# Layer 2's units: matrices further ahead, taps on another queue, x normalized earlier, norms behind the next product, larger runs; and q, k, v from tiles that are loaded first

## The chip, the cores and the metric

The kernel runs on one NeuronCore of a Trainium2 chip. A core has five engines that run side by side, each with its own in-order queue: TensorE (PE, with its weight loads shown as PEld), VectorE (DVE), ScalarE (ACT), GpSimd (POOL) and SyncE (SP), which here only issues DMAs. DMAs can be issued from the queues of SP, ACT and POOL, and all of them run on the same 16 DMA engines. The metric is device time in microseconds (us), lower is better.

## The reference, cut to what matters

x has the shape (4, 384, 64, 64), in float32. Four layers follow each other, each with its input added back: `x = x + layer(group_norm(x))`. Layer 0 is attention over the 4096 positions, on the first 96 channels; layer 1 is a gated product with a filter in the Fourier domain; layer 3 is a depthwise convolution with computed kernels. The change touches the start of layer 0 and most of layer 2:

```python
# layer 0, its start: xn is normalized over the 96 channels of x[:, :96]
qkv = jnp.einsum('oc,bchw->bohw', w_qkv, xn)     # and a batch norm with given statistics
# layer 2
y3 = _bn(_dw(x, c3_w, 1), c3_g, c3_b)            # depthwise 3x3, then norm over batch and space
y5 = _bn(_dw(x, c5_w, 2), c5_g, c5_b)            # depthwise 5x5, the same
y1 = x * c1_w.reshape(1, -1, 1, 1) + c1_b.reshape(1, -1, 1, 1)
tok = _bn(kw[:, 0:1] * y3 + kw[:, 1:2] * y5 + y1, ar_g, ar_b)
...
h1 = _gelu(_bn(_pw(tok, cm_w1), cm_g1, cm_b1))   # then a second product, and gates
```

The norms of layer 2 take their mean and variance from all batches and positions of a channel, so y3 and y5 must be known whole for a channel before the sum can be formed.

## The kernel before, in words

The program is written as a list of operations on named tiles. A scheduler orders them on each engine by its own estimate of times, places tiles in buffers, and sets the semaphores. The order of the source is therefore a priority, not a fixed order; but once it is made, each engine's queue runs strictly in order, and an instruction that waits holds all behind it.

**The start (phase_a, x_norm, qkv).** `x_norm(0)` (L631) loads all 24 tiles of batch 0 (3 groups of 128 channels, 8 blocks of 512 positions), measures each with `bn_stats`, and works out mean and scale of every group of channels. `score_shifts` (L714) follows; it holds a branch on a value that is known only at run time, and nothing crosses that branch. Then `qkv` (L680) loads the first 96 channels a second time, block by block (`centered`, L645), and makes q, k and v.

**Layer 2's first half (phase_b, L1138).** The 384 channels are cut into 12 units of 32. In a unit, partitions stand for (batch, channel). For two channels at a time, a pair, `conv53` (L1297) makes both convolutions as six products of z, which holds x with positions on the partitions, with banded matrices. Around these products stand:

- `matrices53` (L1277) makes the matrices of a pair from taps and a mask: even pairs on VectorE, odd ones on GpSimd. They are made two pairs ahead and have four buffers. `taps53` (L1271) loads the taps of four pairs at once, from SP's queue.
- `unit_strips(u + 1)` (L1215) loads the next unit's x (from SP), normalizes it on ScalarE in halves, and, from unit 4 on, transposes it into z on TensorE. It takes one step at every odd n of the 16 pairs. A load or a normalization stands in the same step as the transposes that need it.
- `conv53` copies its result from PSUM into `d_o`, measures it (`bn_stats`), and stores it to memory every fourth pair from ACT's queue: one tensor for 5x5 and one for 3x3.
- `conv_norms` (L1330), at the end of a unit, works out scales and shifts for y3 and y5 with ten small matmuls and a chain through VectorE and ScalarE.
- `unit_tok(u - 1)` (L1366) takes one step at every even n: it loads the convolutions of the unit before as (batch, channel) rows, with runs of 512 bytes, forms the sum in `d5`, with its statistics, and stores it to `tok`.

After the last unit come its tokens, the statistics over all units (`tok_stats`), and the next stage (phase_ef), whose first large products need both.

Of the kernel before, what the change touches and what calls it, by code (L numbers as in the profile page):

```python
# [28 lines left out]
NJ = 3  # L29
# [11 lines left out]
UNITS = C // 32  # L41

# [238 lines left out]
class _Builder:  # L281
    def __init__(self, ctx, tc, ins, out):
# [32 lines left out]
        self.d53 = [  # L315
            [self.dram.tile([32, B, 32, P], F32, tag=f"d{i}{u}", name=f"d_{i}_{u}") for u in range(UNITS)]
            for i in range(2)
        ]
# [189 lines left out]
    def phase_a(self, strips):  # L508
# [3 lines left out]
        with ExitStack() as ctx:  # L512
# [8 lines left out]
            self.probs = attention.enter_context(tc.tile_pool(name="a_probs", bufs=2, side="right"))  # L521
            self.center = self.const(cp, "center", PD)
# [8 lines left out]
            for k in ("r0", "m0", "n0"):  # L531
                setattr(self, k, cp.tile([P, NJ, B], F32, tag=k, name=k))
            self.qkv_weights(cp)
            for _ in self.x_norm(0):
                pass
# [6 lines left out]
            for _ in self.qkv(0, q, k4, vt):  # L542
                pass
# [87 lines left out]
    def x_norm(self, b):  # L631

        st = self.stats_tile("x_st")
        for i in range(8):
            for j in range(NJ):

                x = self.wk("x_in", "xs", 2) if b else self.big.tile([P, 512], F32, tag="q", name="x_in0", bufs=9)
                self.nc.sync.dma_start(x, self.ins["x"][b][:, j, i * 512 : (i + 1) * 512])
                self.nc.vector.bn_stats(st[:, j, i, :], x)
            yield 0.5  # L640
# [4 lines left out]
    def centered(self, b, i):  # L645
# [4 lines left out]
        nc.sync.dma_start(x, self.ins["x"][b][0:PD, 0, i * 512 : (i + 1) * 512])  # L650
        nc.vector.tensor_scalar(
            x, x, self.m0[0:PD, 0, b : b + 1], self.r0[0:PD, 0, b : b + 1], ALU.subtract, ALU.mult
# [27 lines left out]
    def qkv(self, b, q, k4, vt):  # L680
# [3 lines left out]
        xc[0] = self.centered(b, 0)  # L684
        yield 1.0
        xn[0] = self.layer_norm(xc[0])
        xc[1] = self.centered(b, 1)
        yield 2.0
        for i in range(8):
            if i + 2 < 8:  # L690
                xc[i + 2] = self.centered(b, i + 2)
                yield 1.0
# [34 lines left out]
    def maxima(self, b):  # L727
# [3 lines left out]
        q = []  # L731
        k = [self.probs.tile([P, 2048], F32, tag="p", name="mx_k") for _ in range(2)]
        for i in range(8):
# [3 lines left out]
            q.append(self.big.tile([P, 512], F32, tag="q", name="mx_q", bufs=9))  # L737
# [400 lines left out]
    def phase_b(self):  # L1138
# [5 lines left out]
        with ExitStack() as ctx:  # L1144
# [12 lines left out]
            for n in range(4):  # L1157
                self.matrices53(n)
# [4 lines left out]
            self.unit_x = [[] for _ in range(UNITS)]  # L1163
            for u in range(UNITS):
                st = self.bt_p.tile([P, 2, 16, 6], F32, tag="st", name="st")
                strips = self.unit_strips(u + 1) if u + 1 < UNITS else iter(())
                tok = self.unit_tok(u - 1) if u else self.unit_strips(0)
                nets = iter(()) if u else self.nets(cp)
                for n in range(16):
                    if u or n > 1:  # L1170
                        self.matrices53(16 * u + n + 2)
                    self.conv53(u, n, st)
                    next(strips if n % 2 else tok, None)
                    if n % 3 == 2:
                        next(nets, None)
                self.conv_norms(u, st)
# [38 lines left out]
    def unit_strips(self, u):  # L1215
# [3 lines left out]
        for i in range(2):  # L1219
            x = self.bx_p.tile([P, 2048], F32, tag="x", name="unit_x")  # L1220
            for b in range(B):
                nc.sync.dma_start(
                    x[32 * b : 32 * b + 32], self.x1[b][32 * q : 32 * q + 32, j, i * 2048 : (i + 1) * 2048]
                )
            self.unit_x[u].append(x)
            for h in range(4):
                if h % 2 == 0:
                    xh = x[:, 512 * h : 512 * h + 1024]
                    nc.scalar.activation(
                        xh, xh, AF.Identity, bias=self.norm_u[:, 1, u : u + 1], scale=self.norm_u[:, 0, u : u + 1]  # L1230
                    )
                if j:
                    m = self.pm("strip_m")
                    for k in range(4):
                        at = (4 * h + k) * P
                        nc.tensor.transpose(m[:, k * P : (k + 1) * P], x[:, at : at + P], self.ident)
                    at = 1 + 16 * i + 4 * h
                    zv = self.z[:, 32 * q : 32 * q + 32, at : at + 4, :]
# [796 lines left out]
```

## Time and profile before

| | us |
|---|---|
| median of 3 runs | 4879.94 |
| the runs | 4866.37 to 4882.83 |
| the profiled execution | 4868.55 |
| its span | 4866.7 |

| stage of the span | from, us | to, us | what |
|---|---|---|---|
| start | 0 | 41 | statistics, weights, branch |
| layers 0 and 1 | 41 | 2478 | attention, the Fourier products |
| layer 2's units | 2478 | 3041 | 12 units: first product to last |
| between | 3041 | 3088 | last tokens, statistics, gates |
| the rest | 3088 | 4867 | layer 2's large products, layer 3 |

The page divides the span in 40 slices and gives each engine's busy share in tenths. A row of a group or of the timeline names the line, the engine, the operation and its tiles, and, in brackets, how long the engine was idle before it and what ended that. Rows of waits give the total us, how often, and the longest. TensorE is busy 91% of the span, VectorE 60%, ScalarE 41%, GpSimd 15%. In the window of the units the DMA engines moved 172.50 MB in 133,702 packets, of which 104,916 were under 2 KB.

### The profile page before, as it was taken

How to read it: one execution, taken by the hardware profiler on the slowest of the kernel's cores; microseconds unless marked ns; L12 is line 12 of the kernel's file. 1: busy time of each engine (PE TensorE's matmuls, PEld its weight loads, DVE VectorE, ACT ScalarE, POOL GpSimd, SP SyncE). 2: the span in 40 equal slices, each digit the busy share in tenths (PEclk: the TensorE clock that was granted, in tenths of full speed). 3: DMA queues.
4: the chain of work that ended last, by engine and by line, in shares of the span. 5: the costliest groups of instructions: out<-in, count | busy, mean ns of one | idle time of the engine just before them, and what ended most of it. 6: DMA issues, size and time to landing. Idle time of an engine off the chain costs nothing. (4 is left out here: it accounts for less than half of the span.)

```text
span 4866.7 us, 49663 instructions
## 1 busy us (share of the span) xinstructions
PE 4413.5 (91%) x18441; PEld 2456.1 (50%) x18441; DVE 2901.2 (60%) x4642; ACT 1998.2 (41%) x2974; POOL 728.9 (15%) x594
## 2 busy tenths in 40 slices
PE   6899999999999999988978889699999997778888
PEld 2233444344443444435468888344444443667888
DVE  6766566655566455566867778555521113667898
ACT  3454344444444443436345556211133334753321
POOL 1000000000000000000034445000000001225544
PEclk8999999999999999999989989899999998788999
DMA  4211212121211111113259999866664444895776
GB/s 159 79 51 48 80 65 72 46 79 33 75 55 67 48 52 52 64 51 124 73 176 296 280 286 308 279 254 253 239 236 151 156 156 160 314 341 185 230 255 232
DMA packets 345857, 749.23 MB, mean 154 GB/s; under 512 B 22684, under 2 KB 172295, under 8 KB 336647
## 3 DMA queue, kind: packets, MB, share of 16 engines
q1 hardware_dynamic: 279864, 471.92, 31.3%
q0 software_dynamic: 32640, 151.28, 7.9%
q10 hardware_dynamic: 33102, 122.77, 6.5%
q8 instruction: 149, 2.44, 0.2%
q14 instruction: 102, 0.83, 0.1%
HBM read 443.62 MB, written 302.25 MB: 153 GB/s over the span
## 5 line engine op out<-in xcount | busy, mean ns | idle before, releaser
L788 ACT ACTIVATE probs<-sc_s 128x1024 f32<-128x1024 f32 x512 | 496.8, 1020 | 690.6 <-PE av L898 588.2
L898 PE MATMUL av<-probs,vt 128*128 128x512 f32 x1536 | 714.9, 602 | 0.0
L1097 DVE SCALAR_TENSOR_TENSOR acc<-band,vecs,acc 128x512 f32<-128x512 f32 x708 | 496.4, 746 | 45.2 <-POOL band L1058 40.0
L1591 PE MATMUL h_m<-f_h,cm_w_t 128*128 128x512 f32 x1152 | 497.4, 595 | 7.4 <-ACT f_h L1579 7.4
L1308 PE MATMUL conv_m<-toep,z 128*128 128x192 f32 (+1 forms) x2304 | 447.0, 356 | 17.8 <-DVE toep L1289 17.6
L898 PEld LDWEIGHTS av<-probs,vt 128*128 128x128 f32 x1536 | 275.6, 191 | 338.1 <-issue 334.4
L1308 PEld LDWEIGHTS conv_m<-toep,z 128*128 128x128 f32 x2304 | 410.9, 198 | 41.0 <-issue 10.1
L1905 PE MATMUL conv_m<-toep,z 128*128 128x128 f32 x3072 | 393.6, 286 | 37.9 <-POOL toep L1892 19.6
L1905 PEld LDWEIGHTS conv_m<-toep,z 128*128 128x128 f32 x3072 | 379.3, 202 | 39.9 <-POOL toep L1892 19.9
L1537 PE MATMUL h_s<-e_tok,cm_w_t 128*128 128x512 f32 x768 | 363.3, 596 | 4.2 <-DVE e_tok L1522 4.2
L1591 PEld LDWEIGHTS h_m<-f_h,cm_w_t 128*128 128x128 f32 x1152 | 219.8, 191 | 285.0 <-issue 273.9
L780 PE MATMUL sc_s<-q,k 32*128 32x512 f32 x2048 | 310.7, 644 | 19.4 <-ACT probs L788 19.1
L1599 DVE BATCH_NORM_STATS2 h_st<-f_h 128x6 f32<-128x512 f32 x96 | 66.4, 693 | 429.9 <-ACT f_h L1598 429.9
L1289 POOL TENSOR_TENSOR toep<-w,band 128x1280 f32<-128x1280 f32 x94 | 272.2, 2900 | 307.0 <-PE conv_m L1308 201.1
L1020 PE MATMUL t_m<-w_in_t,xb 128*128 128x384 f32 x768 | 279.7, 499 | 4.3 <-DVE coef L1037 4.1
L934 PE MATMUL proj_m<-xm,w_proj_t 128*128 128x512 f32 x576 | 271.6, 611 | 4.9 <-DVE xm L873 4.9
L1544 ACT COPY e_h<-h_s 128x1024 f32<-128x1024 f32 x96 | 97.2, 1012 | 400.3 <-PE h_s L1537 400.3
L1546 DVE BATCH_NORM_STATS2 h_st<-e_h 128x6 f32<-128x512 f32 x192 | 123.5, 685 | 203.8 <-ACT e_h L1544 203.8
L1537 PEld LDWEIGHTS h_s<-e_tok,cm_w_t 128*128 128x128 f32 x768 | 146.6, 191 | 188.7 <-issue 183.3
L941 DVE SCALAR_TENSOR_TENSOR x_res<-proj_m,bn_c,x_res 128x512 f32<-128x512 f32 x96 | 71.8, 748 | 241.0 <-PE proj_m L934 240.8
L1020 PEld LDWEIGHTS t_m<-w_in_t,xb 128*128 128x128 f32 x768 | 143.3, 193 | 142.0 <-issue 60.7
L1537 PE MATMUL h_s<-z,cm_w_t 128*128 128x512 f32 x384 | 196.1, 592 | 0.0
(408 smaller groups left out, 6383.4 us busy)
## 6 DMA issues: line engine op xcount, KB each, us to landing
d<-d_o ACTq DMA_DIRECT2D x96, 512.0 KB
c_d<-d SPq DMA_DIRECT2D x96, 512.0 KB
hid<-e_h ACTq DMA_DIRECT2D x16, 3072.0 KB
f_h<-hid SPq DMA_DIRECT2D x16, 3072.0 KB
x_in<-in_x SPq DMA_DIRECT2D x96, 256.0 KB
x_res<-in_x SPq DMA_DIRECT2D x32, 768.0 KB
xa<-x_res POOLq DMA_DIRECT2D x32, 768.0 KB, 3.7
xa_out<-xa SPq DMA_DIRECT2D x32, 768.0 KB
```

The lines of the kernel that those rows point to most:

```text
L780: nc.tensor.matmul(s[:, g], lhsT=k4[32 * g : 32 * g + 32, c], rhs=q[i][32 * g : 32 * g + 32], start=True, stop=True,)
L788: nc.scalar.activation(p[:, h * 1024 : (h + 1) * 1024], s[:, 2 * h : 2 * h + 2].rearrange("p a b -> p (a b)"), AF.Exp, scale=0.25,)
L898: nc.tensor.matmul(av[0], lhsT=vt[:, 4 * c + v, :], rhs=p[:, v * 512 : (v + 1) * 512], start=c == 0 and v == 0, stop=c == 7 and v == 3,)
L934: nc.tensor.matmul(m, lhsT=self.w_proj[:, j, o * P : (o + 1) * P], rhs=xm[:, j], start=j == 0, stop=j == NJ - 1,)
L1020: nc.tensor.matmul(m[:, 0:C], lhsT=xb[:, j], rhs=self.w_in[:, j, :], start=j == 0, stop=j == NJ - 1,)
L1097: nc.vector.scalar_tensor_tensor(out, src(j, k), w, done, ALU.mult, ALU.add)
L1289: eng.tensor_tensor(t, self.w53[:, at : at + 160].rearrange("p (m n) -> p m n", n=8).unsqueeze(2).to_broadcast([P, 20, 8, 8]), band.rearra ...
L1308: nc.tensor.matmul(m[:, c * 256 + to : c * 256 + to + 64 * (k1 - k0)], lhsT=self.z_[:, at : at + P], rhs=t[:, 10 * c + k0 : 10 * c + k1].r ...
L1537: nc.tensor.matmul(s[:, v, :], lhsT=w1[:, j, o * P : (o + 1) * P], rhs=t[j][:, v * 512 : (v + 1) * 512], start=j == 0, stop=j == NJ - 1,)
L1546: nc.vector.bn_stats(st[:, o, 8 * b + 2 * i + v, :], h[:, o, v * 512 : (v + 1) * 512])
L1591: nc.tensor.matmul(m, lhsT=w2[:, o, j * P : (j + 1) * P], rhs=h[:, o, v * 512 : (v + 1) * 512], start=o == 0, stop=o == 5,)
L1905: nc.tensor.matmul(m[:, ch * P : (ch + 1) * P], lhsT=self.z_[:, at : at + P], rhs=t[:, 8 * c + 2 * i : 8 * c + 2 * i + 2].rearrange("p m a ...
```

## The change

Layer 2's units: `LEAD = 3` sets the matrices three pairs ahead, with five buffers, and five are made before the first pair. The taps' loads are issued from GpSimd's queue and have three buffers instead of two. `unit_strips` becomes a generator that loads and normalizes one step before it yields; the first step of unit u + 2 is taken at the end of unit u, and each load is cut in two along the positions. `conv_norms` of a unit is called behind the first pair of the next one. The token steps are taken at n = 2, 4, ..., 14 and 15 instead of 0, 2, ..., 14. The two convolutions lie beside each other in one tensor, `d_o` and `d53` alike, so that a store writes 8 KB a row and a load reads runs of 1 KB; the sum is written over the unit's x (`o`) instead of over `d5`, and stored from there.

The start: eight tiles (the first 128 channels) are loaded first of all and kept; `first_norm` works out mean and scale of the 96 channels alone; after the branch, `qkv` reads the kept tiles; the other 16 tiles are measured behind it. In `maxima`, inside the branch, q takes another buffer.

```diff
+LEAD = 3
-        self.d53 = [
-            [self.dram.tile([32, B, 32, P], F32, tag=f"d{i}{u}", name=f"d_{i}_{u}") for u in range(UNITS)]
-            for i in range(2)
-        ]
+        self.d53 = [self.dram.tile([32, B, 32, 2, P], F32, tag=f"d{u}", name=f"d_{u}") for u in range(UNITS)]
...
+            self.x0_st = self.stats_tile("x1_st")
+            self.x0 = self.first_tiles(self.x0_st)
             self.center = self.const(cp, "center", PD)
...
             self.qkv_weights(cp)
-            for _ in self.x_norm(0):
-                pass
+            self.first_norm(self.x0_st)
             self.score_shifts(cp)
...
-            for _ in self.qkv(0, q, k4, vt):
+            for _ in self.qkv(0, q, k4, vt, self.x0):
+                pass
+            for _ in self.x_norm(0, self.x0_st):
                 pass
...
+    def first_tiles(self, st):
+        tiles = []
         for i in range(8):
+            x = self.big.tile([P, 512], F32, tag="q", name="x_in0", bufs=9)
+            self.nc.sync.dma_start(x, self.ins["x"][0][:, 0, i * 512 : (i + 1) * 512])
+            tiles.append(x)
+        for i, x in enumerate(tiles):
+            self.nc.vector.bn_stats(st[:, 0, i, :], x)
+        return tiles
...
-    def centered(self, b, i):
+    def centered(self, b, i, src=None):
         x = self.wk("ln_x", "lx", 2)[0:PD]
-        nc.sync.dma_start(x, self.ins["x"][b][0:PD, 0, i * 512 : (i + 1) * 512])
+        if src is None:
+            src = x
+            nc.sync.dma_start(x, self.ins["x"][b][0:PD, 0, i * 512 : (i + 1) * 512])
...
-            for n in range(4):
+            for n in range(LEAD + 2):
                 self.matrices53(n)
...
+            strips, behind = self.unit_strips(1), None
+            next(strips)
             for u in range(UNITS):
...
                 for n in range(16):
                     if u or n > 1:
-                        self.matrices53(16 * u + n + 2)
+                        self.matrices53(16 * u + n + LEAD)
                     self.conv53(u, n, st)
-                    next(strips if n % 2 else tok, None)
+                    if n == 0 and u:
+                        self.conv_norms(u - 1, behind)
+                    if n % 2:
+                        next(strips, None)
+                    elif n or not u:
+                        next(tok, None)
+                    if n == 15 and u:
+                        next(tok, None)
...
+                    if n == 15 and u + 2 < UNITS:
+                        strips = self.unit_strips(u + 2)
+                        next(strips)
-                self.conv_norms(u, st)
+                behind = st
+            self.conv_norms(UNITS - 1, behind)
...
+        load(0)
+        norm(0)
+        yield
+        for n in range(8):
+            i, h = n // 4, n % 4
+            x = tiles[i]
+            if j:
...
+            if n == 0:
+                load(1)
+            if n % 2 and n < 7:
+                norm(n // 2 + 1)
+            yield
...
-            self.w53_ahead = self.bt_p.tile([P, 8 * 80], F32, tag="w53", name="w53")
+            self.w53_ahead = self.bt_p.tile([P, 8 * 80], F32, tag="w53", name="w53", bufs=3)
-            self.nc.sync.dma_start(self.w53_ahead, src.rearrange("p c m n -> p (c m n)"))
+            self.nc.gpsimd.dma_start(self.w53_ahead, src.rearrange("p c m n -> p (c m n)"))
-        t = self.bt_p.tile([P, 20, 8, 8], F32, tag="toep", name="toep53", bufs=4)
+        t = self.bt_p.tile([P, 20, 8, 8], F32, tag="toep", name="toep53", bufs=LEAD + 2)
...
-            for v in range(2):
-                nc.scalar.dma_start(
-                    self.d53[v][u][:, :, 2 * n - 6 : 2 * n + 2].rearrange("y b c n -> (y b) (c n)"),
-                    self.d_o[:, v].rearrange("p c n -> p (c n)"),
-                )
+            nc.scalar.dma_start(
+                self.d53[u][:, :, 2 * n - 6 : 2 * n + 2].rearrange("y b c v n -> (y b) (c v n)"),
+                self.d_o.rearrange("p c v n -> p (c v n)"),
+            )
...
+            d = self.bc_p.tile([P, 8, 2, P], F32, tag="d", name="c_d")
+            o = self.unit_x[u][i // 2][:, i % 2 * 1024 : i % 2 * 1024 + 1024]
+            nc.sync.dma_start(
+                d.rearrange("p y v n -> p y (v n)"),
+                self.d53[u][8 * i : 8 * i + 8].rearrange("y b c v n -> (b c) y (v n)"),
+            )
...
-            nc.sync.dma_start(self.tok[u, :, :, sl].rearrange("b c n -> (b c) n"), d5)
+            nc.sync.dma_start(self.tok[u, :, :, sl].rearrange("b c n -> (b c) n"), o)
```

## What it does to the time: the prediction

> **What bounds the kernel now.** I read the 40 slices first, then windows of 40 us over layer 2's units, then who TensorE waited for there, then single rows for durations.
>
> ```profile
> PE 6899999999999999988978889699999997778888
> DVE  6766566655566455566867778555521113667898
> PEclk8999999999999999999989989899999998788999
> DMA  4211212121211111113259999866664444895776
> ```
>
> TensorE (PE) is the engine of nearly every slice. It dips in the first slices and from the 21st to the 26th (2433 to 3163 us). There the DMA digit goes to 9, where it is 1 to 3 before. Two windows of that stage and TensorE's waits in it (line waited for: us in total, times, longest):
>
> ```profile
> 2840.00:2880.00 40.00, 35.75 (x190) 33.09 (x189) 30.09 (x64) 22.84 (x51) 18.26 (x8) 0.91 0.93 292
> 2960.00:3000.00 40.00, 36.59 (x212) 34.03 (x210) 34.28 (x70) 27.35 (x59) 20.45 (x8) 1.00 1.02 317
> ```
>
> ```profile
> PE strip_m L1236 <- ACT unit_x L1229: 24.7, 10, 3.0
> PE conv_m L1308 <- DVE toep L1289: 17.6, 7, 4.9
> PE cn_m L1350 <- DVE z L1241: 6.2, 5, 3.8
> PE cn_rep L1341 <- DVE st L1322: 5.9, 4, 1.9
> PE strip_m L1236 <- ACT z L1243: 5.4, 8, 0.9
> PE cn_rep L1341 <- DVE z L1241: 3.5, 3, 1.2
> ```
>
> ```profile
> POOL toep L1289 <- DMA w<-in_c_t: 55.0, 13, 7.9
> ```
>
> The columns after the length are the busy us of PE, PEld, DVE, ACT and POOL, then granted clock, DMA share, GB/s. TensorE stands still some 65 us, in three families: strips that wait for x to be normalized or for the copy into z (30.1), products that wait for their matrices (17.6), and the norms at a unit's end (17.4 with three small rows). The reader is to see also that the DMA engines are full (0.93 to 1.02) while TensorE is not.
>
> What would a unit cost without waits? Two rows of the chain:
>
> ```profile
> 2883.44 0.87 PE strip_m L1236 x8
> 2885.90 16.89 PE conv_m L1308 x94
> ```
>
> 94 matmul records in 16.89 us is 0.180 each; a pair of channels has 12, so 2.16 us. 192 pairs make 414 us; 256 strip transposes at 0.109 make 28; the norms' ten matmuls a unit (0.45 and twice 0.5 us) make 17. Together 459. The products began at 2478.1 and ended at 3040.9: 562.8, or 46.9 a unit. So 104 us are lost: 65 in gaps, and the rest in the clock, whose 14 windows from 2480 to 3040 average 0.93 (7% of 560 is 40 us). The granted clock is halved for 3.4 to 10 us just behind such gaps: at 3000 us, behind a gap of 2.7, 14 records took 4.4 us instead of 2.5.
>
> **The change, part by part.**
>
> *Norms behind the next product* (17.4 us of gaps). Nothing is added; ten matmuls a unit move behind the new unit's first pair, 2.16 us of cover, while the last statistics (ACT copies 0.37 and 0.38, two DVE rows of 0.42) take 1.6. The chain then runs through ACT and DVE, whose queues hold other work, so I leave 4. The tokens, first at n=0, start at n=2; their loads no longer stand on SP waiting for the last d store, which lands some 7 us after its issue (SP waited 103.3 us there in all).
>
> *Matrices three ahead* (17.6). LEAD goes from 2 to 3, the buffers from 4 to 5: a matrix is made 2.16 us earlier. The slack to its buffer's last reader is unchanged, since there was one pair of slack and there is one. A fifth matrix is made ahead of the stage by DVE: 1.48 us, between 0 and 1.5 on the path, as z's copies follow on DVE at 2470.9; I take 1. Unit 0's gap of 4.9 belongs to the small nets and stays: 12 go.
>
> *Taps on GpSimd's queue.* 48 DMA issues leave SP, where they stood behind loads waiting for stores (POOL waited 55 us for taps). On GpSimd the nearest row is the band store at L1124: 0.72 us to issue, 3.9 to landing. That is 2.9 us a unit on POOL, which is busy some 23 of 47. Behind an issue that waits for its buffer stand POOL's own multiplies, and TensorE waits for those; with three buffers the reader it waits for is two matrices back. The skill speaks against it: "SBUF — State Buffer", "two separate sides", warns that a DMA issued from GpSimd starves while VectorE runs a two-port operation, and gives 620 ns becoming about 3100. By that rule a tap comes 2.5 us late, and where all four of a unit were exposed this would cost 12 × 4 × 2.5 = 120 us. By the rows, 32 band stores beside a VectorE two thirds busy were issued in 718 to 727 ns, with landings of 3.8 to 5.4. Nor are VectorE's rows in the units the SBUF copies that the page means. I take the rows, and no cost: taps are fetched a group ahead, 8.6 us.
>
> *x a step ahead* (30.1). The same 48 normalizations and 256 transposes; each load is cut in two, 192 of 128 KB instead of 96 of 256. SP keeps 288 issues (192 + 48 + 48 against 96 + 96 + 48 + 48). A normalization (1.24 us) now stands two loop steps ahead of its transpose, 4.3 us: this covers the 2.2 to 3.0 of each gap. The risk is the load. The tokens are now written into unit_x, so a tile comes free only when its store has landed, not when ACT has read it. A load that waits stands on SP with the d loads and token stores behind it. The second half is wanted at n=7, some 13 us after its issue at n=1; landings under load took 7 to 8. I take 20 of the 30.
>
> *Larger runs.* d becomes one tensor: 48 stores of 1 MB instead of 96 of half, 48 loads in 1 KB runs instead of 96 in 512 B. In the packet records 90,112 packets of 512 B took 31 ns in the mean, 0.31 of the DMA engines' time there. For 1 KB the nearest row is a store of zeros at the start, 46 ns; the 2 KB rows take 84 (median). Taking 46 for two times 31, the stage's DMA share of 0.92 loses 0.08, from 43.3 us a unit to 39.5. "DMA: Bandwidth & Descriptors", Specifications, says that line rate needs only 512 B; by that nothing is won and the floor stays at 43.3. The rows disagree: 27 ns (median) for 512 B is 19 B/ns, against 22 at 1 KB and 26 at 4 KB. I take the rows.
>
> *Sum of the units.* The gaps give 13 + 12 + 20 = 45, and the clock in proportion (45/65 of 39) 27: 72, or 40.9 a unit. But the new DMA floor of 39.5 lies so near that both cannot be met; I take 42.0. 12 × (46.9 − 42.0) = **59**. Ends: 25 (the old floor, 44.8 with its latencies) and 95 (almost all of the 104).
>
> *The tail.* From the last product (3040.9) to the next stage's first (3087.8) the chain is d store, d load, tokens, statistics. VectorE waited 9.5 us for the first d load, and the 4 MB came until 3069.8. The loads' packets occupy 0.408 of 40 us; at 46 against 62 ns that saves 4 us, and a d tile is free after ACT's square, not after a store: **5** (2 to 8), less the 1 of the head.
>
> *Sooner q, k, v.*
>
> ```profile
> 30.19 0.37 DVE L621 BATCH_NORM_AGGREGATE gn_mv<-x_st 128x2 f32<-128x48 f32 x1
> ...
> 38.21 1.48 SPq L650 DMA_DIRECT2D ln_x<-in_x  x2
> ...
> 41.08 0.54 DVE L651 TENSOR_SCALAR ln_x<-ln_x,m,r 96x512 f32<-96x512 f32 x1 [6.51 <-DMA ln_x<-in_x]
> ```
>
> Before, 24 tiles are loaded and measured, then comes the branch (34.4 to 38.2), then x is loaded again; TensorE works in earnest from 41 on. After, eight tiles suffice and go first on SP: issue at 2.1 instead of 4.0, so the first lands at 7.1 (9.1 before) and the eighth seven times 0.85 us later (24 tiles landed within 9.1 to 29.5), at 13.1. Statistics 0.7, the chain of the norm 4.2 (30.2 to 34.4), the branch 3.8, no second load: 22 against 41, 19 us sooner. The other 16 tiles are measured later, 16 × 0.69 = 11 us of DVE where it is 71% busy (60 to 160 us): I give back 4. **15** (6 to 20).
>
> Sum: 59 + 5 − 1 + 15 = 78. The profiled execution took 4868.55 (span 4866.7); 4790.5 after. The median of the three runs is 11.4 above that execution, so the median to come is **4802**.
>
> **The rivals.**
>
> *The DMA engines are the wall.* For it: shares of 0.93 to 1.02, and more bytes per us are asked for (13.9 MB a unit; at the best window's 317 GB/s that is 43.8 us). Against it: the last unit, with the d and token traffic but no x loads, ran its products with no gap but at the first pair in 36.9. Units at 44.8 give 25: 25 + 4 + 15 = 44, so 4836.
>
> *SP's queue closes up (slower).* The second load of a unit waits for the landing of a token store, and behind it stand the d loads that VectorE's token steps need; VectorE holds the matrices behind those. If the store lands later than the load's slack of 13 us, the excess is paid in every unit. At 50, three us more than now, the units lose 36 and the start and tail give 19: 17 slower, 4897. It decides from an excess of 6.5 us a unit over my forecast (78/12). Against it: landings of 7 to 8 us now.
>
> *The start is not sooner.* VectorE runs in order; if the 16 later tiles are scheduled ahead of the first norm, its chain waits for their loads, as now. Then 15 becomes 2: 4815.
>
> *All of it goes*: 95 + 20 + 6 = 121, so 4759.
>
> **How the numbers follow.** Forecast 0.55, DMA wall 0.20, start not sooner 0.10, all goes 0.08, SP closes up 0.05, no difference 0.02. The range 4755 to 4848 holds the first four but for their edges, with the wall's own spread of some 12. A measurement of this kernel tells 0.3% (15 us) from no change. Faster takes the first four nearly whole, 0.92; same 0.04 (the 0.02, and the wall with a failed start); slower 0.04, nearly all of the fifth case.
>
> **What would show it.** TensorE's waits in the units: the rows of unit_x, of toep and of cn_rep and cn_m shrink to about 20 us in all, and the mean clock there goes over 0.96. The DMA share stays above 0.9 with over 310 GB/s. The first centered x comes at 20 to 26 us; from the last product to the next stage is 42 us, not 47. I am wrong if the units stay at 45 us, or if TensorE gets a new wait behind SP's loads of x or d.

## The result, and the profile after

| | before | after |
|---|---|---|
| median, us | 4875.09 (7 runs) | 4844.08 (7 runs, 4833.05 to 4848.91) |
| ratio, 95% interval | | 0.9932 (0.9921 to 0.9944) |
| span of the profiled execution, us | 4866.7 | 4839.6 |

The kernel is 31 us faster; 78 were forecast. Where the 31 lie is read from points that both traces have:

| point | before, us | after, us | difference |
|---|---|---|---|
| first centered x | 41.1 | 25.2 | −15.9 |
| first scores | 61.6 | 41.3 | −20.3 |
| 129th score product | 206.1 | 177.4 | −28.6 |
| first product of the units | 2478.1 | 2460.2 | −17.9 |
| last product of the units | 3040.9 | 3011.4 | −29.5 |
| first product of the next stage | 3087.8 | 3067.7 | −20.0 |
| end | 4866.7 | 4839.6 | −27.1 |

The start gave more than forecast. The units, from which 59 were to come, gave 11.6, and the tail behind them took 9.4 back. Of the 28.6 us at the 129th score product 17.9 are left at the units. Some 8 of the difference lie in layers 0 and 1: from that product to the last statistics before the units these traces took 2250.3 and 2258.6 us. In the seventeen kernels with the new start (those below included), whose TensorE order is the same up to there, this stretch takes 2250.7 to 2259.8, so these traces do not lay it to the edits. The other 2.3 us lie in the entry to the units, and belong to the change.

First the page's 40 slices of the changed kernel:

```profile
PE   6999999999999999989987898699999997778888
DVE  7766556645656455556867777555521113767898
PEclk9999999999999999989988999899999998788999
DMA  4312212111211111113168898776664444995776
```

In TensorE's 21st slice, where units 0 and 1 lie, the digit rose from 7 to 8; in the 22nd, with units 2 and 3, it fell from 8 to 7. Three windows show the bad place, each from the first product of a unit (2, 3 and 9) to that of the next. The columns are as in the prediction's windows.

```profile
2535.89:2571.59 35.70, 35.70 (x204) 34.08 (x203) 33.48 (x70) 20.94 (x50) 25.54 (x13) 1.00 0.91 329
2571.59:2640.59 69.00, 44.01 (x238) 40.33 (x236) 44.80 (x92) 40.13 (x80) 27.23 (x14) 0.79 0.95 309
2880.69:2926.19 45.50, 42.04 (x236) 39.27 (x236) 36.20 (x73) 29.02 (x62) 25.56 (x12) 0.95 0.90 299
```

Units 0 to 2 transpose no strips and run with one wait of 1.3 us, in 37.1 us on average (45.1 before). Unit 3, the first that transposes strips for its successor, takes 69.0 (50.8 before). Units 4 to 10 take 47.3 on average (48.5 before); 42.0 were forecast. So units 0 to 2 won 24 us, unit 3 lost 18 of them, units 4 to 10 won some 8, and unit 11 lost 3. TensorE's waits in the units:

```profile
PE strip_m L1294 <- ACT unit_x L1280: 43.1, 14, 15.3
PE conv_m L1370 <- DVE z L1299: 9.4, 4, 6.9
PE cn_rep L1402 <- DVE st L1384: 6.8, 4, 2.1
PE cn_rep L1402 <- DVE z L1299: 4.6, 4, 1.2
```

The row of matrices (17.6 us) is gone. The wait for the normalized x, which was to shrink from 24.7, grew to 43.1: in unit 3 from 4.8 to 24.4, and in units 4 to 10 it stayed, 19.9 before and 18.7 after. Where x is held up stands in SP's own waits:

```profile
SPq L1463 <- DVE st L1384: 165.3, 31, 11.7
SPq L1272 <- DMA d<-d_o: 68.2, 12, 20.3
SPq L1272 <- DMA tok<-unit_x: 52.9, 18, 6.4
```

L1463 is the store of the tokens, L1272 the load of x. SP stands 165 us in front of token stores whose sum VectorE has not made, with the loads behind it; then the loads wait for landings of such stores and of stores of d. (The first row names the statistics `st`, which start on VectorE as the sum ends. For the store below the sum ends at 2902.65 us.) A piece of SP's timeline, start and duration:

```profile
2894.61 4.49 SPq L1272 DMA_DIRECT2D unit_x<-x  x4
2902.68 0.34 SPq L1463 DMA_DIRECT2D tok<-unit_x  x1
2903.07 9.94 SPq L1272 DMA_DIRECT2D unit_x<-x  x10
```

The effect at the same unit's end, in TensorE's timeline:

```profile
2912.62 7.09 PE L1370 MATMUL conv_m<-toep,z 128*128 128x256 f32 x38
2919.54 1.04 PE L1294 MATMUL strip_m<-ident,unit_x 128*128 128x128 f32 x8
2920.41 0.82 PE L1370 MATMUL conv_m<-toep,z 128*128 128x192 f32 x4
2923.53 1.09 PE L1294 MATMUL strip_m<-ident,unit_x 128*128 128x128 f32 x8 [2.30 <-ACT unit_x L1280]
2925.78 0.69 PE L1402 MATMUL cn_rep<-st,mean 128*128 128x64 f32 x2 [1.15 <-DVE z L1299]
2926.27 3.72 PE L1370 MATMUL conv_m<-toep,z 128*128 128x256 f32 x12
```

The reader is to see three things. The last strips of the next unit come behind the unit's last pair and wait for x. The first of the norms' products (cn_rep) stand in front of the next unit's first pair, not behind it, although the source has them behind: that pair needs the last strip in z. That the scheduler put them ahead for this reason is inferred here; moving the strips, below, tests it. And behind the gaps a pair takes 3.72 us instead of 2.16: the granted clock is 0.50 for 3.4 us.

### The profile page after: what moved, and what is told of

Read it like the earlier page. It is cut to its first block, busy times and chain, and to the rows that moved or that the text cites. A ratio compares the mean times of both kernels' runs of the same rounds, so it can differ in the third digit from the quotient of the medians.

```text
span 4839.6 us, 49747 instructions
## 1 busy us (share of the span) xinstructions
PE 4399.5 (91%) x18445; PEld 2453.7 (51%) x18445; DVE 2892.0 (60%) x4647; ACT 1996.9 (41%) x2976; POOL 757.7 (16%) x643
## 4 chain that ended last, share of the span: by engine, by line
PE 32%; DVE 7%; DMA 6%; ACT 3%; issue 2%; POOL 1%; SPq 0%; ACTq 0%; DVEq 0%; POOLq 0%
PE h_m L1658 10%; PE h_s L1604 10%; PE conv_m L1370 6%; PE conv_m L1972 2%; DMA c_d<-d 2%; DMA wmix<-in_mix_t 1%; DMA g_h<-h 1%; DVE toep L1959 1%; PE box_m L2050 1%; DVE in_x L2052 1%; DMA ax<-x 1%; DVE in_x L2062 1%; DMA unit_x<-x 1%; DVE box L2034 0%; ACT g_h L1908 0%
## 5 line engine op out<-in xcount | busy, mean ns | idle before, releaser
L1370 PEld LDWEIGHTS conv_m<-toep,z 128*128 128x128 f32 x2304 | 408.5, 197 | 31.6 <-DVE z L1299 10.1
L1051 PEld LDWEIGHTS t_m<-w_in_t,xb 128*128 128x128 f32 x768 | 144.4, 194 | 141.6 <-issue 62.5
```

What stands on the lines that cost most here:

```text
L1051: nc.tensor.matmul(m[:, 0:C], lhsT=xb[:, j], rhs=self.w_in[:, j, :], start=j == 0, stop=j == NJ - 1,)
L1370: nc.tensor.matmul(m[:, c * 256 + to : c * 256 + to + 64 * (k1 - k0)], lhsT=self.z_[:, at : at + P], rhs=t[:, 10 * c + k0 : 10 * c + k1].r ...
```

## The experiments

Each kernel is the changed one with the edit shown, but for the first two rows and start_only. "Units" is first to last product in its profiled execution, "tail" from there to the first product of the next stage. Two cautions on single traces: the units begin at 2449 to 2483 us in kernels whose TensorE order is the same up to there, so lengths of stages are compared and not their places; and before and start_only, whose units have the same code, take 562.8 and 569.4 us, so less than 7 us between two rows of that column says nothing.

| kernel | ratio to before (95%) | units, us | unit 3 | units 4 to 10, mean | tail |
|---|---|---|---|---|---|
| before | 1 | 562.8 | 50.8 | 48.5 | 46.8 |
| changed | 0.9932 (0.9921, 0.9944) | 551.2 | 69.0 | 47.3 | 56.3 |
| start_only | 0.9942 (0.9925, 0.9959) | 569.4 | 49.6 | 48.8 | 47.3 |
| tok_act | 0.9900 (0.9871, 0.9930) | 554.7 | 70.9 | 48.0 | 47.5 |
| halves | 0.9922 (0.9893, 0.9951) | 548.9 | 64.2 | 48.0 | 56.7 |
| no_defer | 0.9902 (0.9874, 0.9929) | 548.2 | 75.1 | 46.9 | 54.2 |
| own_sum | 1.0000 (0.9988, 1.0013) | 580.9 | 69.0 | 51.9 | 64.7 |
| own_act | 0.9931 (0.9903, 0.9958) | 557.0 | 68.1 | 48.3 | 52.1 |
| no_defer_act | 0.9889 (0.9856, 0.9922) | 533.4 | 62.9 | 45.9 | 47.0 |
| lead2_act | 0.9922 (0.9900, 0.9944) | 553.5 | 70.8 | 47.6 | 47.3 |
| whole | 0.9918 (0.9889, 0.9947) | 554.0 | 67.8 | 48.0 | 48.8 |
| whole_nd_act | 0.9862 (0.9831, 0.9892) | 534.5 | 65.2 | 45.6 | 47.1 |
| za_nd_act | 0.9865 (0.9835, 0.9895) | 536.0 | 63.8 | 46.0 | 46.8 |
| hp_za_whole_nd_act | 0.9940 (0.9923, 0.9958) | 566.1 | 60.2 | 50.5 | 46.5 |
| s13 | 0.9902 (0.9884, 0.9920) | 537.9 | 69.7 | 46.0 | 49.2 |
| s13_nd_act | 0.9885 (0.9866, 0.9903) | 527.0 | 66.7 | 44.3 | 50.0 |
| s13_whole_act | 0.9861 (0.9842, 0.9881) | 528.5 | 67.0 | 44.2 | 50.2 |
| s13_whole_nd_act | 0.9856 (0.9835, 0.9878) | 512.5 | 63.0 | 42.6 | 48.2 |

**The start alone.** The kernel before with `first_tiles`, `first_norm` and the tiles handed to `qkv`; the units as before.

> The kernel before with only the edit of the first norm and the sooner q, k, v. Theory A (the start brings nearly all of the change, and what layer 2's units win by 11.6 us their tail loses by 9.4): the first scores come 20 us sooner, the attention is 28 us ahead at the 128th score row, the first product of the units 18 to 20 us sooner, and the end is 18 to 27 us sooner, a ratio of 0.9945 to 0.9963. Theory B (start and units share the 31 us, as the forecast's sum has it, 15 from the start): 15 us sooner, ratio 0.997, and the units account for the rest.

28 us (0.58% of 4875; the interval is 20 to 37) of the 31 are here; against the changed kernel the ratio is 0.9990, with an interval that holds 1. The attention is 28.5 us ahead at the 129th score product, as in the changed kernel. Theory A holds: the edits of the units, all together, won nothing that the times can show.

**Why is x late: SP's order, the sum in place, or the divided loads?**

```diff
 tok_act
-            nc.sync.dma_start(self.tok[u, :, :, sl].rearrange("b c n -> (b c) n"), o)
+            nc.scalar.dma_start(self.tok[u, :, :, sl].rearrange("b c n -> (b c) n"), o)
 halves: self.bx_p bufs=6 of [P, 2048] -> 12 of [P, 1024], tiles[n // 2] in the strips
 own_sum
-            o = self.unit_x[u][i // 2][:, i % 2 * 1024 : i % 2 * 1024 + 1024]
+            o = self.bc_p.tile([P, 1024], F32, tag="sum", name="c_sum", bufs=2)
 (and the b_c pool from 3 to 2 buffers, for the space)
 own_act: own_sum with the store of tok_act
 whole
-            for k in range(2):
+            x loads of 2048 columns, four for a tile instead of eight
```

> The changed kernel with the token stores issued from ScalarE's queue behind the square instead of from SP's. Theory A (x comes late because SP's loads of x and d stand behind token stores that wait for VectorE's sum, 165 us of waiting in the units): units 3 to 10 lose most of their gaps for unit_x, the units take 530 us or less instead of 551, and the whole about 4822. Theory B (the late x comes from the landing of the token store in the same tile, not from the queue): the gaps move to the load's own wait and stay, 551 within 6 us, 4844. Theory C (the DMA engines are the wall): also 4844, with a DMA share over 0.95 in every window. Theory D (ScalarE's 48 issues of 0.35 us each, 17 us, delay the copies out of PSUM that TensorE needs): over 4850.

> The changed kernel with each x tile of 2048 columns split into two tiles of 1024, 12 instead of 6 of them in the same space, so that a half comes free when its own token store has landed. Theory B (x is late because the tile waits for the landing of its last token store): the gap of 15.3 us in unit 3 and the regular 2.3 us of units 7 to 10 go, the units take 525 to 535 us instead of 551, the whole about 4825. Theory A (SP's queue behind the stores): a gain under 8 us. Theory C (DMA wall): none, 4844.

> The changed kernel, but the token sum goes to a tile of its own (two of 4 KB, paid for with the third d tile), so that an x tile is free as soon as ScalarE has read it and no load of x waits for a token store's landing. Theory B (the sum in place is what makes x late): the loads of x move from 3 to 11 sixteenths of the unit to the unit before and its start, TensorE's waits for the normalized x fall from 43 us to under 10, the units take 530 us or less. Theory A (it is SP's order: loads stand behind stores that wait for VectorE): waits of 30 us or more stay and the units take 545 to 555. A cost in either case: with two d tiles instead of three the tail is 3 to 6 us longer.

> The sum in a tile of its own and the token stores on ScalarE's queue, both. If A and B each hold a part, this has no wait for x except at unit 3; then what is left is the wait of the norms for VectorE's last statistics at the unit's end. Theory F (the regular 5.4 us gap of the kernel with stores on ScalarE's queue comes from VectorE's order, not from x): that gap stays at 4 to 6 us in units 4 to 10, the units take 545 to 555 us and the whole 4825 to 4835. Rival (the gap was a consequence of late x or of the tile's reuse): the gap goes and the units take 520 us, the whole 4800.

> The changed kernel with the x loads undivided again: 96 of 256 KB instead of 192 of 128 KB. Every issue of a hardware DMA waits in the program for the one eight issues before it, SP's and ScalarE's counted together, and in the changed kernel SP's x loads wait 68 us for stores of d that have nothing to do with x. Theory L (the divided loads use up these eight places, so that loads and token stores stand behind stores of 1 MB): that wait falls under 35 us, x comes sooner, the units take 535 us or less, the whole about 4828. Rival (the order behind the token stores, theory A, is all): units 545 to 555, the whole 4844, and a little slower where a half of x could have been used before the other.

The position of the loads answers first. In sixteenths of the unit in which the strips are wanted, the first load of unit 10's x is issued at 3.2 in the changed kernel and its second tile at 10.1; the source has them at 15 of the unit before and at 1. In own_sum they stand at 3.5 and 9.0, though the sum is no longer in place: theory B falls as the main cause (not cleanly, since two d tiles instead of three cost time of their own: tail 64.7). In halves the tile comes free earlier, and nothing is gained but 5 us in unit 3. With the store on ScalarE's queue the same loads stand at 13.3 of the unit before and at 4.6. So it is SP's order that makes x late, as theory A has it. TensorE's waits in tok_act:

```profile
PE cn_rep L1402 <- DVE st L1384: 39.8, 8, 6.1
PE strip_m L1294 <- ACT unit_x L1280: 19.4, 2, 15.8
PE conv_m L1370 <- ACT d_o L1381: 4.8, 2, 4.6
```

The wait for x is left in unit 3 alone, and another has taken its place, so that the units are no shorter: 554.7 us, where theory A had 530 or less. What tok_act won is in the tail: 47.5 instead of 56.3, where unit 10's last token store is issued 9.4 us into the tail and not 19.9. Its ratio overlaps the changed kernel's. own_act, with the sum apart as well, keeps the new wait (28.5 us for the statistics) and its units take 557.0, so that wait is no consequence of late x or of the sum in place.

whole tests a third reading of the wait rows: the program gives hardware DMAs eight semaphores in turn, SP's and ScalarE's together, and an issue waits for the DMA that had its semaphore before. That is how a load of x can wait for a store of d. With half the loads this row fell from 68.2 us (12 waits) to 52.4 (3 waits), not under the 35 of theory L, and the tail to 48.8, but the units did not change (554.0): this is not what kept them long.

**The new wait, at the unit's end.** tok_act and its VectorE there:

```profile
2925.04 1.04 PE L1294 MATMUL strip_m<-ident,unit_x 128*128 128x128 f32 x8
2931.49 0.69 PE L1402 MATMUL cn_rep<-st,mean 128*128 128x64 f32 x2 [5.41 <-DVE st L1384]
2932.45 4.00 PE L1370 MATMUL conv_m<-toep,z 128*128 128x256 f32 x10 [0.28 <-DVE z L1299]
```

```profile
2925.30 1.49 DVE L1351 TENSOR_TENSOR toep<-w,band_p 128x1280 f32<-128x1280 f32 x1 [2.16 <-issue]
2926.70 0.74 DVE L1451 SCALAR_TENSOR_TENSOR unit_x<-c_d,cn_s,tok_m 128x512 f32<-128x512 f32 x1
...
2928.70 0.74 DVE L1449 SCALAR_TENSOR_TENSOR tok_m<-c_d,cn_s,tok_m 128x512 f32<-128x512 f32 x1
...
2929.69 0.73 DVE L1451 SCALAR_TENSOR_TENSOR unit_x<-c_d,cn_s,tok_m 128x512 f32<-128x512 f32 x1
...
2930.34 1.09 DVE L1384 BATCH_NORM_STATS2 st<-d_o 128x6 f32<-128x256 f32 x3
2931.35 1.05 DVE L1299 COPY z<-strip_m 128x512 f32<-128x512 f32 x1
```

VectorE works through without a pause from 2925.3, with token steps ahead of the last statistics (2930.34) and of the strip's copy into z (2931.35), which the norms and the next product need. Six kernels vary this:

```diff
 no_defer (and no_defer_act with tok_act's store)
-                    if n == 0 and u:
-                        self.conv_norms(u - 1, behind)
...
-                    if n == 15 and u:
-                        next(tok, None)
...
+                    next(strips if n % 2 else tok, None)
...
+                self.conv_norms(u, st)
 lead2_act: tok_act with LEAD = 2 and bufs=LEAD + 3 for toep53 (five, as with LEAD = 3)
 za_nd_act: no_defer_act with nc.scalar.copy for every strip
 whole_nd_act: no_defer_act with the loads of whole
 hp_za_whole_nd_act: all of these, and high priority for the statistics at n == 15
```

> The changed kernel with the norms back at the unit's end and the tokens back at the even steps from 0, everything else as changed. By the forecast (the deferral wins 13 us in the units): about 13 us slower than the changed kernel there, and the tail unchanged. Theory E (in units with strips the deferral wins nothing, since the last strips hold TensorE at the unit's end, while it puts the tokens two steps later, so that the tail has unit 10's last tokens ahead of unit 11's): the tail from the last product to the next stage falls from 56 to 46 us, the units change by less than 6, the whole is 5 to 12 us faster than the changed kernel, near 4835.

> Norms at the unit's end, tokens at the even steps, and the token stores on ScalarE's queue. Theory F: with no token step at the 15th pair VectorE has one step (1.5 us and its statistics) less in front of the last statistics, the gap at the unit's end falls from 5.4 to about 3.5 us and the half clock behind it stays; units 540 to 546, tail 47, the whole about 4820. If the two gains of the kernels with one of the edits (stores 13 us, norms 14 us, both against the changed kernel's median) add up: 4817. If they are the same gain: 4830.

> Matrices two pairs ahead as before, but still five buffers, and the token stores on ScalarE's queue. Theory F (with three ahead in five buffers a matrix on VectorE waits for the pair two back to end, 2.2 us at the unit's end, and the last statistics stand behind it): with one more pair of slack that wait goes, the regular gap falls from 5.4 to 3 us or less, and the half clock behind it gets shorter, so units 5 to 10 take 44 us or less instead of 47.8 and the whole about 4810. Rival G (the lead of three is what removed the 17.6 us of waits for matrices): these come back, 10 to 18 us, and the whole is 4831 or more. Rival H (it is the amount of VectorE's work at the unit's end, tokens bunched there): the gap stays above 4.5 us.

> The token stores on ScalarE's queue, norms at the unit's end, tokens at the even steps, and the copy of every fourth strip into z on ScalarE (0.58 us) instead of VectorE (1.05 us). Theory H (VectorE's queue at the unit's end, two token steps with the last statistics and the copy of the last strip behind them, is what is left in the way): the next product no longer waits for VectorE's copy, the rows of z on VectorE go, and the gaps of 4 to 6 us at the ends of units 4 to 10 fall below 3; units 520 us or less, the whole about 4800. Rival (the statistics alone set it): gaps stay within 1 us, 4813.

> Undivided x loads, the token stores on ScalarE's queue, norms at the unit's end, tokens at the even steps. Theory L: it wins a further 8 to 15 us over the kernel without the first of the three, 4800 or less. Rival (with the stores gone from SP's queue the loads are soon enough anyway): the same as without it within 6 us, 4813; what remains is VectorE at the unit's end and unit 3.

> All of these together, and the last pair's statistics of each unit given priority over the tokens on VectorE. If the three causes (SP's order, VectorE's copy, VectorE's statistics behind tokens) are separate, the units come to about 500 us with unit 3 still above 60, and the whole to 4785. If the unit's work on VectorE and the catching-up of unit 3 set the time, it is 4800 to 4810, no better than the best of the others.

no_defer refutes the deferral's 13 us: without it the units are 548.2, not longer. Theory E was right on that and wrong on the tail (54.2, not 46). In lead2_act the gap is still 5.41, so the wait for a matrix's buffer is not it, theory F falls; nor do waits for matrices come back, so it was not the third pair of lead that removed them (whether the fifth buffer did it or the taps' queue was not tried apart). In no_defer_act the units take 533.4, but its profiled execution is the fastest of its four, and by the intervals it can't be told whether the gains of tok_act and no_defer add up in it or are one. za_nd_act (536.0) and whole_nd_act (534.5) are each within its interval, as their rivals had it and not the 520 of theory H. In the kernel with everything together x is loaded earliest of all (10.3 of the unit before, then 0.5) and units 4 to 10 still take 50.5: at the ends of the last of them the norms wait 4.83 us for statistics and the next product 2.74 more for the strip. The priority did not do its work: at one such end two token operations (2881.81 and 2882.80 us) still stand on VectorE in front of the last statistics, which end at 2885.19. The time is worse than either expectation for it. It says that x in time is not enough, and leaves open whether VectorE's order is all that is left.

**The place of the last strip.**

```diff
 s13 (SLOTS = (1, 3, 5, 7, 8, 10, 11, 13))
-                    if n % 2:
+                    if n in SLOTS:
                         next(strips, None)
-                    elif n or not u:
+                    if n % 2 == 0 and (n or not u):
                         next(tok, None)
 s13_whole_act, s13_nd_act, s13_whole_nd_act: the same with the edits above
```

> The changed kernel with its deferred norms, undivided x loads, token stores on ScalarE's queue, and the eight strips of the next unit at pairs 1, 3, 5, 7, 8, 10, 11 and 13 instead of at every odd one up to 15. Theory K (the deferral fails because the next product itself needs the last strip's copy): the next unit's first pair follows the 15th at once, the gaps of 4 to 7 us at the ends of units 4 to 10 and the half clock behind them go, these units take 43 us or less, the whole about 4790. Rival H (VectorE has too much to do at the unit's end in any case): TensorE waits as long for matrices or for the norms, units over 46, the whole 4810 to 4830.

> The same with the norms at the unit's end in the source and the tokens at the even steps. Theory K: the norms need not be deferred in the source, since the scheduler puts the next product in front of them once its strips are ready; as fast as the kernel with the deferral or up to 10 us faster, since tokens come a step sooner: 4780 to 4795. Rival H: 4810.

> The same with the x loads still divided in two. Theory L (the eight places for DMAs in flight): 5 to 10 us slower than with undivided loads. Rival (the halves come sooner and that pays): equal within 4 us or faster.

> The changed kernel with nothing but the strips two pairs sooner, the token stores still on SP. Theory A with K (both needed): x is still late, so the strips wait for it in the middle of the unit instead of at its end, 40 us or more in all for the normalized x; the whole within 12 us of the changed kernel, 4832 to 4856. If K alone is the cause of the lost gain: 4815 or less.

Theory K holds in its mechanism. In s13_whole_nd_act the scheduler puts the next unit's first pairs in front of the norms by itself. Its timeline at such a border, and two windows of 42 us in it:

```profile
2860.70 8.82 PE L1363 MATMUL conv_m<-toep,z 128*128 128x256 f32 x48
2870.82 0.45 PE L1395 MATMUL cn_rep<-st,mean 128*128 128x64 f32 x2 [1.29 <-DVE st L1377]
2871.10 3.45 PE L1363 MATMUL conv_m<-toep,z 128*128 128x256 f32 x18
```

```profile
2822.00:2864.00 42.00, 40.08 (x237) 37.39 (x236) 36.20 (x74) 28.38 (x64) 25.68 (x13) 1.00 0.95 331
2864.00:2906.00 42.00, 40.03 (x236) 37.35 (x235) 36.26 (x74) 26.94 (x59) 25.62 (x13) 1.00 0.98 331
```

The next unit begins near 2865, inside the 48 records without a gap. One gap of 1.29 us is left at the border, and the clock stays at 1.00. Units 6 to 9 take 41.9 to 42.3 us, and the kernel 4801.88, the lowest median of all that were run (s13_whole_act, 4803.61, can't be told from it); its interval lies below the changed kernel's.

In time the theory did less well. Both kernels with undivided loads came between its numbers (4790; 4780 to 4795) and those of rival H (4810 and more). s13 alone is faster than the changed kernel, 0.9902 against 0.9932 with intervals that just do not meet. But with the norms back, the loads whole and the stores moved, the strips' place shortened the units of the trace by 22 us and the ratio only from 0.9862 to 0.9856, well inside the intervals. The profiled execution of s13_whole_nd_act lost 17 us against the changed kernel's before its 129th score product, at half speed (last section); whether its other three did is not known.

s13 shows that both causes count: with the strips' place alone x is still late (45.1 us of waits, 24.6 of them in unit 3, and up to 4.7 us in units 8 and 10) and the units take 537.9; its time lies between its two expectations. s13_nd_act against s13_whole_nd_act speaks for theory L: 12 us of the medians, and no run of the one (4808.56 to 4817.15) falls among those of the other (4799.35 to 4805.24), though the ratios' intervals overlap.

## Why the prediction was wrong

By its own steps, with what each gave:

- **Start, 15 (6 to 20): it gave 28 (20 to 37).** The first centered x was put at 22 us and came at 25.2; the first scores come 20.3 us sooner. The other 8 us up to the 129th score product are the clock, which the sum left out. A window from the first scores on in the kernel before, and one in the changed kernel:

```profile
61.60:100.00 38.40, 37.29 (x79) 14.57 (x78) 21.79 (x41) 15.73 (x24) 2.08 (x4) 0.60 0.30 89
```

```profile
41.30:80.00 38.70, 36.72 (x136) 14.87 (x136) 33.88 (x67) 22.99 (x36) 3.12 (x6) 1.00 0.41 121
```

TensorE is as busy in both, but the clock is 0.60 in the one and 1.00 in the other, and the second finishes 136 matmul records against 79. These 8 us are not the edit's to claim: by the last section, the same start meets a clock now better and now worse than before's. The give-back of 4 did not show, and the rival of a start that is not sooner is refuted.
- **Matrices, 12 of 17.6: right**, and more: TensorE no longer waits for them at all, unit 0's 4.9 us included, which was to stay. The third pair of lead was not needed (lead2_act).
- **Taps on GpSimd, no cost: right within the units, not at their entry.** An issue takes 0.59 us and lands in 6.6 (median); GpSimd waits for taps no more (55.0 us before). But the first matrices wait for the first taps. VectorE's row before, then after:

```profile
2462.50 5.68 DVE L1289 TENSOR_TENSOR toep<-w,band_p 128x1280 f32<-128x1280 f32 x4 [1.51 <-DMA w<-in_c_t]
2446.62 7.08 DVE L1351 TENSOR_TENSOR toep<-w,band_p 128x1280 f32<-128x1280 f32 x5 [5.89 <-DMA w<-in_c_t]
```

  From the last statistics to the units' first product the two kernels with the old units take 21.8 and 19.7 us, the sixteen with the new ones 22.8 to 25.5 (24.1 in the changed kernel). The sum had 1 us for a fifth matrix there, and nothing for later taps.
- **Larger runs, floor of 39.5 a unit: about right.** The DMA share over the units fell from 0.92 to 0.84 at the same 280 GB/s. In three windows of 42.0 us, each about a unit, the best kernel has 0.93, 0.95 and 0.98, which makes 39.1 to 41.2. The rival of the DMA wall at 44.8 is refuted by units of 41.9 to 42.3 us there.
- **x a step ahead, "I take 20 of the 30": this step failed.** The wait for the normalized x grew from 24.7 to 43.1 us, by unit 3, and did not shrink elsewhere. I took the source's places, 15 and 1, for the queue's places. The risk was named (a load that waits holds what stands behind it), but the heavier one was the other way round: loads of x stand behind token stores that wait for VectorE, and the tokens themselves run 6 to 8 sixteenths of a unit later than before (unit 8's four stores went from 5.0, 9.6 and 12.3 of unit 9 and 1.9 of the next to 11.4 and then 1.9, 4.6 and 7.6 of the next). This is a mild form of the rival in which SP's queue closes up, through the order in the queue more than through the landing it named.
- **Norms behind the next product, 13 of 17.4: failed with it.** The product that was to cover them waits for the last strip, and that stands at the 15th pair. I counted 2.16 us of cover without asking what the cover itself waits for. no_defer puts its worth at nothing; in s13_whole_nd_act, with the strips earlier and no deferral in the source, pairs of the next unit do cover the norms.
- **Clock, 27 in proportion to the gaps: nothing.** The mean clock of the units went from 0.93 to 0.92; it followed the gaps, and they stayed: 63.9 us in the four rows above, 63.3 in the six of before. It reaches 0.97 in s13_whole_nd_act.
- **Tail, 5: it took 9.4 instead.** The last tokens of unit 10 are late by the same queue: with only the stores elsewhere (tok_act) the tail is 47.5.
- **Unit 3** has no step in the sum; this term was put at nothing, and it took 18 us. Units 0 to 2 ran ahead at 37.1 us while their tokens were put off: the first token store of unit 0 is issued in unit 2, at 3.6 sixteenths of it. Unit 3 pays with 92 VectorE operations instead of 73 in a usual unit, and 24 us of waits for x. In the best kernel it still takes 63.0.

So the forecast of 78 failed in the units, at two steps: x was not sooner, and the norms were not covered. The clock's 27 and the tail's 5 hung on these. That 4844.08 still lies within the stated range is luck, a start that gave 13 more than its term, and units that gave 47 less. Of the signs named, the first centered x came in time; of the signs of being wrong, units that stay at 45 us came (45.9 each), and in place of a new wait behind SP's loads the old wait for x grew behind SP's stores.

About 7 us come from the last layer (777.1 us before, 770.2 after, 777.3 in start_only, 764 to 771 in every kernel with the units edited). Its source is untouched, and in all these traces every engine has its instructions and DMAs there in the same order, so it is not a new plan. The cause is open. What else stays open: why the tokens of the first units start so late, what unit 3 would be without that, and whether an order on VectorE with the last statistics truly in front would close the gap at the unit's end.

## What to carry to other kernels

Where a scheduler orders the work, a source line moved ahead is only a wish: read from the trace what stands in front of it in its queue, and what its cover waits for in turn. A store that waits for a slow engine does not belong in a queue with loads that others wait for. Of two waits that end at nearly the same place, taking one away need not show until the other is gone too: in the traces, moving the stores, the norms or the whole loads alone changed the units by no more than the 7 us by which single traces differ, moving the strips alone shortened them by 13, and all four together by 39. The whole times are more modest: the four single gains add up to no less than the gain of all.

## What was not expected of the hardware

Some gaps on TensorE cost more than their length. In tok_act each border from unit 5 to unit 10 had 5.41 us of waiting, and the clock was halved for 6.83 us from before the gap's end on. The stretch behind one such gap:

```profile
2931.49:2936.82 5.33, 5.05 (x14) 4.51 (x15) 2.42 (x5) 2.05 (x4) 0.00 (x0) 0.50 0.75 273
```

At half the clock 5.33 us do the work of 2.7, so by this estimate the gap of 5.41 cost some 8 us. Gaps of 1.3 us at the borders of units 7 to 10 in s13_whole_nd_act left the clock at 1.00.

The clock at the start of the program does not follow from the sooner start. All seventeen kernels with the new start have the same TensorE order there, and first scores within 41 to 46 us. From these to the 129th score product ten of them take 135.5 to 136.3 us, four 139.3 to 139.7, one 144.2 and two 153.5 and 153.7; the kernel before took 144.4. The same pair of products in the changed kernel and in the best one:

```profile
44.33 1.12 PE L811 MATMUL sc_s<-q,k 32*128 32x512 f32 x2
55.34 2.07 PE L812 MATMUL sc_s<-q,k 32*128 32x512 f32 x2
```

In the best kernel such pairs take 2.07 us until 87 us, where its first record of the clock stands; before that record its windows show 1.00, so there the products' own lengths are to be trusted. What decides when the full clock comes was not found: TensorE was busy without a gap from 45.7 us on.
